# A planned one-core kernel (conv block, Fourier mixer, FFN): unread products on TensorE, FFN roundings on another engine, and other buffers for the last image

## The chip, the cores and the metric

One Trainium2 chip; the kernel uses one of its cores. The metric is the device time of one execution in microseconds (us). The kernel before was run three times: 4678.52, 4695.46 and 4697.34 us, so its median is 4695.46 us. A separate execution was profiled.

The core's engines work at the same time, each on its own stream of instructions, in order: TensorE (PE in the profile, with its weight loads as PEld) multiplies matrices into PSUM, VectorE (DVE) and ScalarE (ACT) do element-wise work, GpSimd (POOL) here only starts adding DMAs, and SyncE (SP) starts the other DMAs. TensorE's clock can be throttled; the profile gives the clock that was granted as a share of full speed.

## The reference

Input: 32 images of 96 channels, 56 x 56 pixels, float32. What is computed for each:

```python
# layer 0: inverted residual block
h = relu(bn(einsum('oc,bchw->bohw', w1, x)))        # 96 -> 576 channels
h = relu(bn(dwconv3x3(h, wdw)))                     # a 3x3 filter for each channel
x = x + bn(einsum('oc,bchw->bohw', w2, h))          # 576 -> 96
# layer 1: on tokens, t is [32, 3136, 96]
t = to_tokens(x)
t = t + attn(ln(t))     # 96 -> 192, relu, FFT over the tokens, a complex diagonal with relu,
                        # inverse FFT, 192 -> 96
t = t + ffn(ln(t))      # 96 -> 384 -> 96; inputs of both products are rounded to an 8-bit float
                        # (5 exponent, 2 mantissa bits), sums to a 16-bit float
x = from_tokens(t)
```

The two roundings to 8 bits inside the FFN (of the normalised input, and of the hidden values after the relu) are the "FFN roundings" of the title.

## The kernel before

**The stages of an image.** An image is worked in two halves of 28 rows in the conv block (`unit`, `last_channels`, `front`), in two halves of the spectrum in the Fourier mixer (`mid`), and in four quarters of 784 tokens in the inverse transform and the FFN (`back`).

- `unit`: 128 of the 576 channels of a half. Expand on TensorE (L584), relu into `hs` on ScalarE (L594), then the nine taps of the 3x3 filter: the first by ScalarE into `acc` (L610), one or two by ScalarE into `product` (L626), the others by VectorE (L637), and the products are added by a GpSimd DMA (L645). There are 7 `acc` buffers and 3 `product` buffers, each 128 x 1568 float32. `last_channels` does the last 64 channels on TensorE with banded matrices (L686, L722).
- `front`: the 576 -> 96 products and the residual in PSUM tile `pw` (L844, L878), copied out by ScalarE (`xt`, L891), normalised, kept in DRAM (`tdr`), turned, projected to 192 (L963), first step of the Fourier transform (L994), sent to DRAM (`ydr`).
- `mid`: loads a transform matrix `wb` (L1037, one buffer) and the data `yb` (L1045, two buffers), products on TensorE (L1073), the diagonal and the relus on ScalarE and VectorE (L1085 to L1120), the projection (L1159, L1171) and an inverse step (L1198 to L1202), sent to DRAM (`gdr`).
- `back`: loads `wd` (L1248, one buffer), `gd` (L1251, one buffer) and the residual `tt` (L1257, two buffers), the last inverse step on TensorE (L1272), added to `tt` by VectorE (L1277). Then `norm`: seven statistics (L788), eleven operations on 112 x 7 numbers, ten of them on VectorE and the square root on ScalarE (L798), with small tiles under the token `normf` (two sets). Then the first rounding: seven ScalarE instructions of 112 x 96 (L1289) into `u8`. Seven products turn it (L1307), ScalarE copies (`uT`, L1311). For each of three groups of hidden channels: products (L1328), copy to float16 on ScalarE (L1340), bias and relu on VectorE (L1346), second rounding on ScalarE (L1352, 128 x 784). Then the second FFN product (L1369), a copy (L1378), a bias (L1381), the sum with the residual on TensorE (L1388, which reads `tt` and lets it go, and L1399), a copy (L1404) and the store (L1407).

**What sets the order.** All of that is recorded as steps, each with an engine, a cost in us, the steps it follows, buffer tokens that it takes and gives back, and a rank. `Plan.emit` then plays the steps through a small event model in which each engine is free or busy: a free engine is given the ready step of lowest rank whose tokens are free. The order in which the model gives them out is the order of the instructions on each engine. Ranks come from `START` and `PACE`: `back` of image i has the rank of the conv block of image i + 3, so that several images are in work at once. The consequence at the end: when the conv block of the last image is done, the four quarters of each of the last three images' `back` remain, beside the last mixers.

**Tiles.** PSUM has three buffers `ps` from a pool, and `pw` is taken from another pool, one buffer, every time `front` needs it (`128, 2, 4, 128`, of which the last 32 columns of each 128 are not used).

## Time and profile before

| | |
|---|---|
| time, median of 3 runs (lowest to highest) | 4695.46 us (4678.52 to 4697.34) |
| the profiled execution: its time | 4682.55 us |
| the profiled execution: span from the first to the last instruction | 4680.7 us |
| mean granted TensorE clock | 0.967 |
| busy: PE, DVE, ACT, POOL | 4397.9, 4299.8, 4170.2, 337.3 us |
| steady images: time from one image to the next | about 140 us |

How to read the profile: the busy time of an engine is given as a sum and a share of the span; a second view cuts the span into 40 equal slices and gives the busy share of each in tenths. Groups of instructions are named by line, engine, operation, output tile and input tiles, with shapes, count, total busy time and mean duration. The chain that ended last is found from the last instruction backwards: at each step to what released it. In the list of waits, a row names who waited, who released it, the total, the number of times and the longest. A window is a stretch in us from the start of the span, with the busy time of each engine in it, the granted clock, and the share of the DMA engines. A float32 product of one instruction in the code is two matmul instructions in the profile, unless it is a transpose.

### The profile page before, as it was taken

The page shows a single profiled execution, that of the slowest core. Times are in us where ns is not written, and L with a number is a line of the kernel's source. Part 1 is how long each engine was busy: PE and PEld are TensorE (multiplying, and loading weights), DVE is VectorE, ACT ScalarE, POOL GpSimd, SP SyncE. Part 2 cuts the span into 40 slices and gives each one's busy share as a digit, 9 for nine tenths or more (in the row PEclk, how much of TensorE's full clock was granted, in tenths as well). Part 3 has the DMA queues.
Part 4 walks back from the last instruction along what each step waited for, and adds up shares of the span by engine and source line. Part 5 has one row for each costly group of instructions (what it writes and reads, how often), then busy time and mean ns, then how long its engine had stood idle before and what let it go on. Part 6 is the DMA issues. An engine that isn't in the chain of part 4 may idle for free.

```text
span 4680.7 us, 85686 instructions
## 1 busy us (share of the span) xinstructions
PE 4397.9 (94%) x33744; PEld 3205.3 (68%) x33744; DVE 4299.8 (92%) x6933; ACT 4170.2 (89%) x5510; POOL 337.3 (7%) x397
## 2 busy tenths in 40 slices
PE   7889999999999999999999999999999999999986
PEld 4567776676676767676777676676776776676774
DVE  8999999999999999999999999999999999999943
ACT  4777999999999999999999999998998999899976
POOL 0000000000000000000000000000000000000000
PEclk7999999999999999999999999999999999999987
DMA  4667777767776767776767777777776776777752
GB/s 97 135 158 172 183 179 171 178 167 171 178 175 166 186 163 185 177 181 167 180 170 176 183 176 169 181 176 171 184 182 166 181 179 163 184 178 175 170 135 78
DMA packets 390887, 789.28 MB, mean 169 GB/s; under 512 B 135600, under 2 KB 236532, under 8 KB 390484
## 3 DMA queue, kind: packets, MB, share of 16 engines
q1 hardware_dynamic: 335028, 479.15, 36.4%
q0 software_dynamic: 55296, 304.64, 33.6%
q8 instruction: 266, 4.36, 0.4%
q14 instruction: 137, 1.12, 0.1%
q10 hardware_dynamic: 160, 0.01, 0.0%
HBM read 286.38 MB, written 192.68 MB: 102 GB/s over the span
## 4 chain that ended last, share of the span: by engine, by line
PE 46%; ACT 14%; DVE 11%; DMA 6%; issue 2%; SPq 0%; POOLq 0%; ACTq 0%; DVEq 0%
PE pw L844 10%; PE ps L584 8%; DVE acc L637 7%; DMA acc<-product 5%; PE ps L722 4%; PE ps L1073 3%; PE ps L994 2%; PE ps L963 2%; PE ps L1369 2%; PE ps L1272 2%; PE ps L1171 2%; ACT acc L654 2%; PE ps L1328 2%; ACT product L626 1%; ACT acc L610 1%
## 5 line engine op out<-in xcount | busy, mean ns | idle before, releaser
L637 DVE SCALAR_TENSOR_TENSOR acc<-hs,wdw,acc 128x1540 f32<-128x1540 f32 (+2 forms) x1664 | 2971.6, 1793 | 27.2 <-ACT acc L610 18.6
L584 PE MATMUL ps<-xs,w1T 96*128 96x406 f32 x2048 | 823.4, 526 | 48.8 <-ACT al L751 11.6
L844 PEld LDWEIGHTS pw<-w2T,acc 128*112 128x112 f32 x7168 | 766.4, 181 | 64.3 <-issue 40.3
L844 PE MATMUL pw<-w2T,acc 128*112 128x96 f32 x7168 | 804.9, 267 | 5.0 <-ACT acc L654 4.8
L626 ACT ACTIVATE product<-hs,wdw 128x1568 f32<-128x1568 f32 (+1 forms) x384 | 609.4, 1591 | 14.5 <-DMA product<-product 14.1
L584 PEld LDWEIGHTS ps<-xs,w1T 96*128 96x128 f32 x2048 | 371.2, 195 | 300.0 <-issue 136.0
L594 ACT ACTIVATE hs<-ps,b 128x812 f32<-128x812 f32 x512 | 478.6, 935 | 97.8 <-PE ps L584 83.2
L645 POOL DMA_DIRECT2D acc<-product x256 | 227.7, 890 | 3306.4 <-DVE acc L637 384.9
L654 ACT ACTIVATE acc<-acc 128x1568 f32<-128x1568 f32 x256 | 386.9, 1512 | 63.8 <-DMA acc<-product 63.5
L610 ACT ACTIVATE acc<-hs,bd,wdw 128x1568 f32<-128x1568 f32 x256 | 435.2, 1700 | 5.5 <-DVE eo L498 5.4
L722 PE MATMUL ps<-hl,band 128*64 128x385 f32 (+3 forms) x3072 | 419.3, 498 | 4.5 <-ACT hs L594 2.3
L963 PE MATMUL ps<-watt,xnT 97*120 97x192 f32 x1792 | 350.3, 341 | 44.3 <-DVE V L1102 31.4
L963 PEld LDWEIGHTS ps<-watt,xnT 97*120 97x120 f32 x1792 | 305.2, 190 | 105.4 <-DVE V L1102 40.2
L1289 ACT ACTIVATE u<-tt,mf,rf 112x96 fp8e5<-112x96 f32 x896 | 346.4, 462 | 6.1 <-DVE mf L820 5.9
L1352 ACT ACTIVATE h<-h 128x784 fp8e5<-128x784 f16 x384 | 329.4, 860 | 22.3 <-DVE h L1346 21.1
L1073 PEld LDWEIGHTS ps<-wb,yb 112*128 112x128 f32 (+1 forms) x3584 | 306.9, 167 | 58.5 <-issue 23.9
L1340 ACT ACTIVATE h<-ps 128x784 f16<-128x784 f32 x384 | 315.4, 824 | 26.8 <-PE ps L1328 25.7
L1073 PE MATMUL ps<-wb,yb 112*128 112x112 f32 (+1 forms) x3584 | 330.7, 273 | 4.0 <-ACT hs L594 1.8
L722 PEld LDWEIGHTS ps<-hl,band 128*64 128x64 f32 (+1 forms) x3072 | 154.7, 135 | 204.1 <-issue 168.8
L1346 DVE TENSOR_SCALAR h<-h,b1q 128x784 f16<-128x784 f16 x384 | 160.8, 419 | 122.0 <-ACT h L1340 119.9
L994 PE MATMUL ps<-z,wa 56*64 56x384 f32 (+1 forms) x2048 | 242.6, 510 | 24.3 <-ACT hs L594 18.2
L1328 PE MATMUL ps<-uT,w1q 96*128 96x392 fp8e5 x768 | 196.9, 341 | 26.5 <-ACT xnT L948 9.5
(148 smaller groups left out, 6395.6 us busy)
## 6 DMA issues: line engine op xcount, KB each, us to landing
acc<-product POOLq DMA_DIRECT2D x256, 784.0 KB, 8.5
product<-product POOLq DMA_DIRECT2D x128, 756.0 KB, 10.7
yb<-ydr SPq DMA_DIRECT2D x256, 294.0 KB
wd<-in_wd_dram SPq DMA_DIRECT2D x128, 349.1 KB
wb<-in_wb_dram SPq DMA_DIRECT2D x64, 686.0 KB
ydr<-ya SPq DMA_DIRECT2D x256, 168.0 KB
xs<-in_x_dram SPq DMA_DIRECT2D x64, 609.0 KB
tdr<-xt SPq DMA_DIRECT2D x64, 588.0 KB
```

The source lines that it names most:

```text
L584: nc.tensor.matmul(u[h][:, j, 0:QW], lhsT=w1T[:, 128 * k : 128 * (k + 1)], rhs=xs[img, s][0:C, at : at + QW], start=True, stop=True,)
L594: nc.scalar.activation(flat[:, 2 * h * QW : 2 * (h + 1) * QW].rearrange("p (j w) -> p j w", j=2), u[h][:, :, 0:QW], AF.Relu, bias=b1[:, k ...
L610: nc.scalar.activation(acc[img, s, k], u["hs"][:, o + up : o + up + R, :], AF.Identity, scale=weight(up, 0), bias=bd[:, k : k + 1],)
L626: nc.scalar.activation(u["p", dr][:, ra:rb, :], u["hs"][:, ra + o + dr : rb + o + dr, :], AF.Copy, scale=weight(dr, 0))
L637: nc.vector.scalar_tensor_tensor(dst, src, weight(dr, dc), dst, ALU.mult, ALU.add)
L654: nc.scalar.activation(acc[img, s, k], acc[img, s, k], AF.Relu)
L722: nc.tensor.matmul(pv[:, :, ca:cb], lhsT=band[rows, j, dc + 1, 64 * o : 64 * o + 64], rhs=H[rows, q : q + 7, ca + dc : cb + dc], skip_grou ...
L844: nc.tensor.matmul(u["pw"][0:SK, t, n % 4, 0:C], lhsT=src[rows, (G * t + n) * SK : (G * t + n + 1) * SK], rhs=rhs, skip_group_check=True, **k,
L963: nc.tensor.matmul(pv[0:PK, q - a, 0:HA], lhsT=xnT[:, q, 0:PK], rhs=watt, start=True, stop=True,)
L994: nc.tensor.matmul(u["y", b][64 * c : 64 * c + n, j, 0 : 2 * HA], lhsT=wa[at, 0:n], rhs=rhs, start=True, stop=True)
L1073: nc.tensor.matmul(o, lhsT=lhsT, rhs=u["wb"][:, G * s + q, :], start=True, stop=True)
L1289: nc.scalar.activation(u["u8"][:, q, :], u["t"][:, q, :], AF.Identity, scale=u["r"][:, q : q + 1], bias=u["m"][:, q : q + 1], saturate=False,)
```

## The change

It has three parts.

1. **Unread products.** `pw` becomes one tile of 128 x 2 x 512, taken once; `front` uses the first 384 columns of each half. A new function `filler` multiplies `ident` by `ident` into the last 128 columns of the first half; nothing reads them. In `Plan.emit`, when TensorE is free in the model, no step is ready for it, steps are still to come, and it was busy for less than 0.75 of the last 3.413 us of the model, a filler is emitted and counted as 0.23 us of TensorE work. One more such product opens the group.
2. **Roundings.** In the `back` of the last three images (`TAIL = 3`) both FFN roundings are VectorE instructions (`tensor_scalar` and `tensor_copy`) in place of ScalarE ones, with costs in the model of 0.16 and 0.34 us.
3. **Buffers for the last image.** The last image's second `mid` takes its `wb` and both `yb` from `acc` buffers, and its quarters 2 and 3 of `back` take `tt` and the small tiles of `norm` from a `product` buffer each.

The instructions that result: 931 fillers and one opening product. Of the fillers, 187 stand before the expansion of the fourth image, 516 between that and the last expansion of the last image, and 228 after it. They come in runs of 1 to 35. On ScalarE 84 + 36 roundings are gone, on VectorE 84 + 36 are new. One load of `wb`, four of `yb` and two of `tt` have another destination. Because the model's clock and its free times change, the order of the steps changes on PE, ACT, DVE and SP in all of the program, not only where a filler stands.

```diff
+SPARSE = 0.75
+FILLER = 0.23
+TAIL = 3
 class Plan:
+    def sparse(self, now):
+        self.recent = [r for r in self.recent if r[1] > now - self.WINDOW]
+        return sum(b - max(a, now - self.WINDOW) for a, b in self.recent) < SPARSE * self.WINDOW
 ...
     def emit(self):
+        work = sum(s.engine == "PE" for s in self.steps)
 ...
                     cost = self.stretched(now, s.cost) if engine == "PE" else s.cost
+                    if engine == "PE":
+                        self.recent.append((now, now + cost))
+                        work -= 1
 ...
+                if engine == "PE" and idle[engine] and work and now > 0 and self.sparse(now):
+                    self.filler()
+                    idle[engine] = False
+                    cost = self.stretched(now, FILLER)
+                    self.recent.append((now, now + cost))
+                    heapq.heappush(events, (now + cost, count, engine, None))
+                    count += 1
 ...
+    pw = psw.tile([128, 2, 512], F32, name="pw", tag="pw")
 ...
+    def spare(name, p, n):
+        t = w1.tile([128, R, S], F32, name=name, bufs={"acc": 7, "product": 3}[name])
+        return t.rearrange("p r c -> p (r c)")[0:p, 0:n]
 ...
     def norm(u, tag, n, p, after, shift, take, give):
         def sums():
+            if "spare" in u:
+                at = G * C
+                u["st"] = u["spare"][:, at : at + 6 * n].rearrange("p (q v) -> p q v", v=6)
+                at += 6 * n
+                u["w"], u["sd"], u["d"], u["r"], *m = (u["spare"][:, at + n * v : at + n * v + n] for v in range(5))
 ...
                 if i % 4 == 0:
-                    u["pw"] = psw.tile([128, 2, 4, 128], F32, name="pw", tag="pw")
+                    u["pw"] = pw[:, :, 0 : 4 * C].rearrange("p t (q c) -> p t q c", c=C)
 ...
     def mid(img, half):
+        last = img == nimg - 1 and half == 1
+            if last:
+                u["wb"] = spare("acc", SK, 2 * G * SK).rearrange("p (k m) -> p k m", m=SK)
+                if last:
+                    u["yb", t] = spare("acc", SK, G * HA).rearrange("p (g h) -> p g h", h=HA)
 ...
     def back(img, h):
+        tail = img >= nimg - TAIL
+        last = img == nimg - 1 and h >= 2
+        TT, NF = ("product", []) if last else ("tt", ["normf"])
+            if last:
+                u["spare"] = spare("product", SK, R * S)
+                u["t"] = u["spare"][:, 0 : G * C].rearrange("p (q c) -> p q c", c=C)
 ...
+                    if tail:
+                        nc.vector.tensor_scalar(o, t, r, m, ALU.mult, ALU.add, saturate=False)
+                    else:
+                        nc.scalar.activation(o, t, AF.Identity, scale=r, bias=m, saturate=False)
+        engine, cost = ("DVE", 0.16) if tail else ("ACT", 0.36)
 ...
+                if tail:
+                    nc.vector.tensor_copy(u["h8"][:, c, :], u["h", c], saturate=False)
+                else:
+                    nc.scalar.activation(u["h8"][:, c, :], u["h", c], AF.Copy, saturate=False)
+            engine, cost = ("DVE", 0.34) if tail else ("ACT", act(784, 0, 0.09))
 ...
+    def filler():
+        nc.tensor.matmul(pw[:, 0, 4 * C :], lhsT=ident, rhs=ident, start=False, stop=False, skip_group_check=True)
+    nc.tensor.matmul(pw[:, 0, 4 * C :], lhsT=ident, rhs=ident, start=True, stop=False, skip_group_check=True)
+    plan.filler = filler
```

More of the change, by code (lines that the diff above doesn't have):

```diff
@@ L167, in __init__ @@
         self.moving = []
+        self.filler, self.recent = None, []
     def stretched(self, now, work):
@@ L771, in chain, with norm @@
         return t
-    def norm(u, tag, n, p, after, shift, give):
+    def norm(u, tag, n, p, after, shift, take, give):
         stt = nc.vector.scalar_tensor_tensor
         def sums():
-            u["st"] = w2.tile([p, n, 6], F32, name=f"st{tag}")
-            u["w"], u["sd"], u["d"], u["r"], *m = (
-                w2.tile([p, n], F32, name=f"{v}{tag}") for v in ("w", "sd", "d", "r") + ("m",) * shift
-            )
+            if "spare" in u:
[4 more added lines that the diff above has]
+            else:
+                u["st"] = w2.tile([p, n, 6], F32, name=f"st{tag}")
+                u["w"], u["sd"], u["d"], u["r"], *m = (
+                    w2.tile([p, n], F32, name=f"{v}{tag}") for v in ("w", "sd", "d", "r") + ("m",) * shift
+                )
             u["m"] = m[0] if shift else None
@@ L798, in root @@
             nc.scalar.activation(u["sd"], u["w"], AF.Sqrt, scale=1.0 / C)
-        t = [step("DVE", 1.12, sums, after, [f"norm{tag}"])]
+        t = [step("DVE", 1.12, sums, after, take)]
         if n > G:
@@ L923, in front @@
         sent[img, s] = step("SP", 0.1, keep, ev, late=written(2 * SK * G * C))
-        t = norm(u, "a", RP, SK, ev, False, [])
+        t = norm(u, "a", RP, SK, ev, False, ["norma"], [])
         for j in range(2):
@@ L1035, in matrix @@
         def matrix():
-            u["wb"] = w1.tile([SK, 2 * G, SK], F32, name="wb")
+            if last:
+                u["wb"] = spare("acc", SK, 2 * G * SK).rearrange("p (k m) -> p k m", m=SK)
+            else:
+                u["wb"] = w1.tile([SK, 2 * G, SK], F32, name="wb")
             nc.sync.dma_start(
@@ L1042, in f @@
             def f():
-                u["yb", t] = w2.tile([SK, G, HA], F32, name="yb")
+                if last:
+                    u["yb", t] = spare("acc", SK, G * HA).rearrange("p (g h) -> p g h", h=HA)
+                else:
+                    u["yb", t] = w2.tile([SK, G, HA], F32, name="yb")
                 for ri in range(2):
@@ L1052, in mid @@
         after = [sent[img, "y", h] for h in range(4)] + mid_set
-        w = step("SP", 0.1, matrix, after[:1], ["wb"], late=read(2 * G * SK * SK))
+        WB, YB = ("acc", "acc") if last else ("wb", "yb")
+        w = step("SP", 0.1, matrix, after[:1], [WB], late=read(2 * G * SK * SK))
         yb = [
-            step("SP", 0.1, load(t), after, ["yb"], ["ydr"] * (half and t), late=read(SK * G * HA))
+            step("SP", 0.1, load(t), after, [YB], ["ydr"] * (half and t), late=read(SK * G * HA))
             for t in range(2)
@@ L1143, in mid @@
                 ["ps", "V", "eo", "brief"],
-                (["yb"] if part == 2 else []) + (["yb", "wb"] if part == 1 else []),
+                ([YB] if part == 2 else []) + ([YB, WB] if part == 1 else []),
             )
@@ L1255, in residual @@
         def residual():
-            u["t"] = w2.tile([SK, G, C], F32, name="tt")
+            if last:
+                u["spare"] = spare("product", SK, R * S)
+                u["t"] = u["spare"][:, 0 : G * C].rearrange("p (q c) -> p q c", c=C)
+            else:
+                u["t"] = w2.tile([SK, G, C], F32, name="tt")
             nc.sync.dma_start(out=u["t"].rearrange("p q c -> p (q c)"), in_=tdr[img][h // 2, :, G * C * (h % 2) : G * C * (h % 2 + 1)])
@@ L1264, in back @@
         res = step(
-            "SP", 0.1, residual, after[:1] + [sent[img, h // 2]], ["tt"], ["tdr"] * (h == 3), late=read(SK * G * C)
+            "SP", 0.1, residual, after[:1] + [sent[img, h // 2]], [TT], ["tdr"] * (h == 3), late=read(SK * G * C)
         )
@@ L1280, in back @@
         t = step("DVE", dve(G * C, 0.06), add, [t], [], ["ps"])
-        t = norm(u, "f", G, SK, [t], True, [])
+        t = norm(u, "f", G, SK, [t], True, NF, [])
         def quantize(a, b):
@@ L1288, in f @@
                 for q in range(a, b):
-                    nc.scalar.activation(
-                        u["u8"][:, q, :],
-                        u["t"][:, q, :],
-                        AF.Identity,
-                        scale=u["r"][:, q : q + 1],
-                        bias=u["m"][:, q : q + 1],
-                        saturate=False,
-                    )
-            return f
-        t = step("ACT", 0.36 * 4, quantize(0, 4), t, ["u8"])
-        t = step("ACT", 0.36 * 3, quantize(4, G), [t], [], ["normf"])
+                    o, t, r, m = u["u8"][:, q, :], u["t"][:, q, :], u["r"][:, q : q + 1], u["m"][:, q : q + 1]
+                    if tail:
+                        nc.vector.tensor_scalar(o, t, r, m, ALU.mult, ALU.add, saturate=False)
+                    else:
+                        nc.scalar.activation(o, t, AF.Identity, scale=r, bias=m, saturate=False)
+            return f
+        engine, cost = ("DVE", 0.16) if tail else ("ACT", 0.36)
+        t = step(engine, 4 * cost, quantize(0, 4), t, ["u8"])
+        t = step(engine, 3 * cost, quantize(4, G), [t], [], NF)
         def turn():
@@ L1351, in f @@
             def f():
-                nc.scalar.activation(u["h8"][:, c, :], u["h", c], AF.Copy, saturate=False)
+                if tail:
+                    nc.vector.tensor_copy(u["h8"][:, c, :], u["h", c], saturate=False)
+                else:
+                    nc.scalar.activation(u["h8"][:, c, :], u["h", c], AF.Copy, saturate=False)
             return f
@@ L1361, in back @@
             p = step("DVE", 0.34, bend(c), [p])
-            ends.append(step("ACT", act(784, 0, 0.09), quantized(c), [p], [], ["h16"]))
+            engine, cost = ("DVE", 0.34) if tail else ("ACT", act(784, 0, 0.09))
+            ends.append(step(engine, cost, quantized(c), [p], [], ["h16"]))
         def outer():
@@ L1413, in back @@
         t = step("DVE", 0.34, shift, [t])
-        t = step("PE", 1.08, total, [t], ["ps", "brief"], ["tt", "y16"])
+        t = step("PE", 1.08, total, [t], ["ps", "brief"], [TT, "y16"])
         t = step("ACT", 0.97, copied_out, [t], [], ["ps"])
```

## The prediction

> **What bounds the kernel now.** I read the page's head and slices first, then windows by stage, then the groups and the chain of the stage that stands out.

> ```profile
> span 4680.7 us, 85686 instructions
> PE 4397.9 (94%) x33744; PEld 3205.3 (68%) x33744; DVE 4299.8 (92%) x6933; ACT 4170.2 (89%) x5510; POOL 337.3 (7%) x397
> ...
> PE   7889999999999999999999999999999999999986
> ...
> DVE  8999999999999999999999999999999999999943
> ACT  4777999999999999999999999998998999899976
> ...
> PEclk7999999999999999999999999999999999999987
> ```

> In the middle three engines are each busy for nine tenths or more: no single one is the limit, and a little time given back on one is mostly met by another. Only the two ends have slack, and there the clock falls too. The windows (us; PE, PEld, DVE, ACT, POOL busy; granted clock; DMA share; GB/s) give sizes:

> ```profile
> 0.00:300.00 300.00, 239.24 (x1460) 156.28 (x1461) 265.60 (x315) 188.70 (x188) 27.92 (x42) 0.85 0.59 128
> 300.00:4430.00 4130.00, 3969.49 (x30990) 2901.62 (x30989) 3928.49 (x6270) 3803.82 (x5024) 308.55 (x354) 0.99 0.73 175
> ```

> ```profile
> 4430.00:4472.00 42.00, 39.83 (x340) 34.08 (x340) 18.68 (x48) 30.31 (x50) 0.86 (x1) 0.92 0.61 146
> 4472.00:4610.00 138.00, 107.78 (x773) 85.39 (x772) 65.40 (x211) 102.99 (x175) 0.00 (x0) 0.85 0.44 118
> 4610.00:4681.00 71.00, 41.58 (x186) 27.95 (x183) 21.58 (x92) 44.41 (x76) 0.00 (x0) 0.62 0.26 73
> ```

> The conv block ends at 4472. The 209 us behind it, "the tail", have no full engine: they are dependent chains. Clock lost (length x (1 - clock)) is 45 us in the first 300, about 50 in the middle (4 us windows summed; the two digits above are too coarse) and 51 in the last 251. PE's idle time is 61, 161 and 62 us in the same three stretches.

> The tail's groups, and its chain (start us, us, what):

> ```profile
> L1289 ACT ACTIVATE u<-tt,mf,rf 112x96 fp8e5<-112x96 f32 x91 | 34.6, 458 | 2.8 <-DVE mf L820 2.7
> L1352 ACT ACTIVATE h<-h 128x784 fp8e5<-128x784 f16 x39 | 32.5, 853 | 6.6 <-DVE h L1346 5.8 <-DVE df L808 0.7
> ...
> L1346 DVE TENSOR_SCALAR h<-h,b1q 128x784 f16<-128x784 f16 x39 | 16.4, 420 | 65.1 <-ACT h L1340 65.0
> ```

> ```profile
> 4473.61 1.38 PE ps L1272 x14
> ...
> 4652.60 2.69 PE ps L1272 x14
> ...
> 4660.55 1.54 ACT u L1289 x4
> 4662.09 0.75 ACT h L1352
> 4662.89 1.47 PE ps L1369 x4
> ```

> The reader is to see that the same 14 matmuls of L1272 take 1.38 us at 4473 and 2.69 at 4652, and that both ScalarE roundings stand on the chain.

> **The change part by part.** The sum is made against the profiled execution: 4682.55 us, of which 4680.7 are the span. It is 13 us under the median of the three runs (4695.46), inside their spread of 19.

> *Part 1, what a filler costs.* Near row: seven float32 products of 112 x 112 (L1073 x14) take 1.55 us on the chain at full clock, 0.22 each; with 128 columns for 112 that is 0.25. So 187 fillers at the front are 47 us, 516 in the middle 129, 228 after the last expansion 57: in each stretch less than PE's idle time. Where a run is as long as the wait that it fills, it costs nothing; that wait is the cover. Without it each costs 0.25 us of PE (0.5 while the clock is halved), and behind it in PE's queue stands the next stage's matmul, and ScalarE waits for that one's eviction. Only three fillers wait for a semaphore (ScalarE's reading of `pw`), so they bring no new waiting.

> *What the clock is worth.* [...]

> Tail: I take the chain's PE pieces from 4430 on and subtract the same piece at full clock: L1272 three at 2.66 against 1.38, 3.9 us; L963 two at 4.8 against 2.28, 5.1; L1159 three at 2.88 against 1.55, 4.0; L1388 eight at 1.31 against 0.81, 4.0; L1369 six, 8.5 in all against 0.82 each, 3.6; L1171 0.9; L1328, L1399 and L945 together 3.5. Sum 25. Some windows will still be slow, since the plan doesn't know where the chip's windows begin: 20. Fillers on the path: 57 us against 62 of idle is tight, and the tail gets shorter; I charge one in seven, 8 us. Net 12.

> Middle: about 20 slow episodes, 50 us of lost clock; the whole chain is 46% PE, so 23 are worth something. One filler in four on work, 129 / 4 x 46%, costs 15. Net 8. The whole order is dealt anew too, which I can't price beyond +-20: 0.5% of the stretch.

> Front: VectorE is busy 266 of 300 us and covers PE; I can tie 7 us of its waits to a slow PE (264 to 272, 240 to 252) and charge 3 for fillers. Net 4. The first run of 24 fillers stands before the first expansion (9.21 us); at half clock it is up to 12 us long, but ScalarE takes that expansion's result at 19.20 only, since it waits on a DMA.

> *Part 2, roundings.* The window from 4430 holds all twelve quarters of the last three images (L1272 x168). ScalarE loses 84 instructions at 0.37 (seven take 2.61 us) and 36 at 0.86: 62 us of its 178. Unknown is VectorE's price. First rounding: seven L788 of the same 96 columns take 1.22 us; I take that, with ends 0.16 (what ten small numbers take) and 0.25 each. Second: nearest is L1346, 784 float16 to float16, 0.42. [...] I take 0.6. VectorE gets 15 + 22 = 37 us more on 106 of 251: it has the room.

> On the chain stand 15.5 us of L1289 and 17.3 of L1352. They become 15.5 x 1.22 / 2.61 = 7.2 and 17.3 x 0.6 / 0.86 = 12.1: gain 13.5. The copies queued behind them on ScalarE (L1340; 65 us of VectorE's waits) go sooner: 4 more. [...] Late next is VectorE: a rounding in front of a mixer's L1102 (1.03 us) now delays it. [...]

> *Part 3, buffers.* SyncE's queue shows what is removed:

> ```profile
> SPq L1248 <- PE ps L1272: 45.8, 11, 11.4
> SPq L1257 <- PE ps L1388: 40.8, 7, 10.1
> ```

> L1257 is the residual that waits for a `tt` to come free; behind it in SP's queue stand stores and the next `wd` and `gd`. The last image's L1272 start at 4616, 4625.5, 4641.3 and 4652.4. `wd` and `gd` for the third are issued at 4628.5, and the two quarters before show 5.6 and 6.4 us from the `gd` issue to L1272: it could start at 4635. The two waits of 15.8 and 11.1 us can then be some 9.5 each, as the first: 8 less; I count 7, ends 0 and 15. The `wb` and `yb` for the last mixer: those loads wait 15 us for PE (L1037, L1045), none of it on the chain: 0, ends 0 and 4.

> *Sum:* tail -12 - 17.5 - 7 = -36.5, middle -8, front -4: -48.5. 4682.55 - 48.5 = 4634. The runs shown lie 4 under to 15 over the profiled execution; the range has room for that.

> **Rivals.** (a) *The clock doesn't follow*: the chip's idle gaps fall elsewhere than the plan's, the granted clock stays near 0.97, and half of the fillers' charge of 8 + 15 + 3 us is left. For it: episodes come irregularly (936, 1384, 1664, 1920) while the plan's fillers are periodic. Against: in the tail runs of 4 to 19 stand in just the gaps of several us. Time: 4682.5 - 17.5 - 7 + 13 = 4671. (b) *Slower*: fillers stand in PE's way. The place is the middle, where PE has 4% idle. All gains without costs are 20 + 23 + 7 + 17.5 + 7 = 75. If PE sets the pace everywhere (not 46%), half of all 932 x 0.25 = 233 us on work costs 116: 4724. Point of turning: a third on work. Against: DVE and ACT are as full as PE and pay part of it. (c) *More than I count*: the middle's chains are PE's wherever the clock falls, all 50 come back, the tail gives its 25 of clock and 30 of rounding, the front its 4: 4682.5 - 50 - 55 - 4 = 4573. (d) *Nothing*: one bound gives way to DVE everywhere, 4683.

> **How the numbers follow.** Likeliest case 0.65 (4605 to 4660 alone), (a) 0.14, (b) 0.05, (c) 0.13, (d) 0.03. A measurement of this kernel tells about 0.5%, 23 us, from no change: faster is under 4672, slower over 4719. Faster: 0.65 + 0.13 + 0.08 of (a) = 0.86. Within: 0.06 of (a), (d), and 0.01 of (b) = 0.10. Slower: 0.04. The range leaves out half of (c) and (b), and the outer edges: 4585 to 4685.

> **What would show it.** Right: clock of the last 70 us at 0.9 or more, in place of 0.62; L1272 x14 near 1.4 us to the end; the second rounding 0.57 to 0.6 on VectorE; about 22 us less from the end of the conv block to the last mixer's store, and 15 less behind that; PE busy up by about 230 less the slow time, while the middle's step from image to image stays at 140 us or falls by 0.3. Wrong: matmuls waiting behind fillers with their data long there; VectorE full in the tail; a second rounding near 1 us; a middle that moves by more than 20 us either way.

## The result, and the profile after

| | before | after |
|---|---|---|
| time, median of 4 runs (lowest to highest) | 4695.49 us (4678.52 to 4697.34) | 4647.06 us (4644.14 to 4653.59) |
| ratio of the means, 95% interval | | 0.9907 (0.9882 to 0.9932) |
| profiled span | 4680.7 us | 4642.4 us |
| mean granted clock | 0.967 | 0.994 |

The median fell by 48.4 us, and the forecast was a fall of 48.5, to 4634 us from a profiled execution of 4682.55. The means fell by 43.8 us and the profiled executions by 38.4, so how near the two falls are depends on which figure is taken. Cut into stages, the profiled spans tell another story. The first stage ends with the fourth copy of a `pw` (line 891 before, 928 after), the tail begins with the last one (the forecast's own cuts were at 300 us and at 4430 to 4472 us, so its row is laid beside these stages only roughly):

| us | first image's conv block | middle | tail |
|---|---|---|---|
| before | 174.8 | 4297.3 | 208.6 |
| after | 192.9 | 4267.9 | 181.6 |
| difference | +18.1 | -29.4 | -27.0 |
| forecast | -4 | -8 | -36.5 |

The page of the kernel after, head and slices:

```profile
span 4642.4 us, 89413 instructions
...
PE 4496.0 (97%) x35608; PEld 3351.9 (72%) x35608; DVE 4335.3 (93%) x7053; ACT 4121.2 (89%) x5390; POOL 339.9 (7%) x397
...
PE   7999999999999999999999999999999999999998
...
DVE  7899999999999999999999999999999999999956
ACT  4677999999999999999999999999999999999854
...
PEclk8999999999999999999999999999999999999999
```

The clock's last two digits are 9 and 9 where they were 8 and 7, and its first is 8 where it was 7. PE is busier by 98 us, though the span is shorter. In the last two slices VectorE has 5 and 6 where it had 4 and 3, ScalarE 5 and 4 where it had 7 and 6. The windows of the kernel after by stage, cut at 4461 (the end of the conv block) and at 4580 (the last mixer's last store), with the columns that the prediction named:

```profile
0.00:300.00 300.00, 255.22 (x1694) 181.16 (x1694) 247.66 (x288) 177.59 (x177) 25.71 (x39) 0.91 0.54 116
300.00:4430.00 4130.00, 4047.05 (x32246) 3005.07 (x32246) 3953.17 (x6312) 3834.16 (x5056) 314.16 (x358) 1.00 0.74 177
4461.00:4580.00 119.00, 110.61 (x962) 94.10 (x960) 85.87 (x275) 69.75 (x104) 0.00 (x0) 1.00 0.50 137
4580.00:4643.00 63.00, 52.16 (x413) 44.80 (x411) 37.61 (x143) 25.57 (x36) 0.00 (x0) 0.99 0.29 80
```

The granted clock is full or within 1% of it everywhere but in the first 300 us. Summed over windows of 4 us from 300 to 4428, the lost clock is 0.4 us; the same sum for the kernel before is 58. The clock's record in the two traces has the values 1.0 and 0.5 alone, and its changes are whole multiples of 3.413 us apart (80 stretches before, 16 after). From the conv block's end to the last mixer's store it is 119 us for 136 (SyncE's last such store is issued at 4607.9), and behind that 62 for 73.

The groups of the kernel after in its last 213 us:

```profile
L1486 PE MATMUL pw<-ident 128*128 128x128 f32 x422 | 54.0, 275 | 0.0
...
L1403 DVE CAST h<-h 128x784 fp8e5<-128x784 f16 x36 | 20.4, 565 | 0.8
...
L1343 DVE TENSOR_SCALAR u<-tt,rf,mf 112x96 fp8e5<-112x96 f32 x70 | 17.9, 323 | 0.4
```

Both roundings are on VectorE at 0.565 and 0.32 us, and the fillers are 54 us of PE. The chain of the kernel after near its end (start, us, what):

```profile
4607.57 0.56 DVE u L1343 x2
...
4609.49 1.45 PE ps L1324 x14
...
4616.26 0.82 PE ps L1423 x4
4617.08 0.67 PE pw L1486 x6
4617.75 1.24 PE ps L1357 x7
...
4620.02 1.38 PE ps L1324 x14
...
4632.59 0.58 DVE h L1403
...
4636.03 0.89 PE pw L1486 x8
4636.92 0.67 PE ps L1442 x7
```

The 14 matmuls of the inverse step (L1324 now) keep to 1.4 us up to the end; before they had grown to 2.69. The reader is also to see the price: at 4617.08 six instructions of fillers and at 4636.03 eight stand on the chain, directly ahead of matmuls that the end needs. Taken over the whole tail, such pieces are 8.9 us. SyncE's waits in the tail of the kernel after (us in total, times, longest):

```profile
SPq L1296 <- PE ps L1324: 32.3, 8, 6.7
...
SPq L1309 <- PE ps L1453: 22.3, 6, 5.9
...
SPq L1309 <- PE ps L1442: 6.6, 2, 3.4
```

From the conv block's end on, before, the loads of `wd` waited 42.1 us for PE and those of the residual 53.4 (27.6 for L1388, 25.8 for L1399, which are L1442 and L1453 now). They wait 32.3 and 28.9.

### The profile page after: what moved, and what is told of

It is laid out like the page before. It is cut to its first block, busy times and chain, and to the rows that moved or that the text cites. A ratio compares the mean times of both kernels' runs of the same rounds, so it can differ in the third digit from the quotient of the medians.

```text
span 4642.4 us, 89413 instructions
## 1 busy us (share of the span) xinstructions
PE 4496.0 (97%) x35608; PEld 3351.9 (72%) x35608; DVE 4335.3 (93%) x7053; ACT 4121.2 (89%) x5390; POOL 339.9 (7%) x397
## 4 chain that ended last, share of the span: by engine, by line
PE 56%; ACT 14%; DVE 14%; DMA 5%; issue 3%; SPq 0%; DVEq 0%; ACTq 0%; POOLq 0%
PE pw L881 14%; PE ps L615 9%; DVE acc L668 7%; PE ps L1118 4%; PE ps L1031 3%; PE ps L1000 3%; PE ps L1324 3%; ACT product L657 3%; DMA acc<-product 3%; PE ps L1216 2%; PE ps L753 2%; PE ps L1378 2%; PE pw L915 2%; PE ps L1423 2%; PE ps L717 1%
## 5 line engine op out<-in xcount | busy, mean ns | idle before, releaser
L615 PE MATMUL ps<-xs,w1T 96*128 96x406 f32 x2048 | 805.3, 515 | 18.7 <-ACT hs L625 13.7
L881 PEld LDWEIGHTS pw<-w2T,acc 128*112 128x112 f32 x7168 | 749.4, 178 | 63.6 <-issue 44.5
L1000 PE MATMUL ps<-watt,xnT 97*120 97x192 f32 x1792 | 334.1, 330 | 16.7 <-DVE V L1147 13.4
L1000 PEld LDWEIGHTS ps<-watt,xnT 97*120 97x120 f32 x1792 | 292.5, 183 | 71.9 <-issue 35.8
L1118 PEld LDWEIGHTS ps<-wb,yb 112*128 112x128 f32 x3528 | 296.6, 165 | 52.2 <-issue 16.0
L1390 ACT ACTIVATE h<-ps 128x784 f16<-128x784 f32 x384 | 315.5, 824 | 15.4 <-PE ps L1378 10.1
L1405 ACT ACTIVATE h<-h 128x784 fp8e5<-128x784 f16 x348 | 298.8, 859 | 34.0 <-DVE h L1396 33.7
L1118 PE MATMUL ps<-wb,yb 112*128 112x112 f32 x3528 | 321.2, 270 | 5.8 <-ACT h L1390 2.5
L1345 ACT ACTIVATE u<-tt,mf,rf 112x96 fp8e5<-112x96 f32 x812 | 315.2, 463 | 0.6 <-DVE mf L857 0.6
L1486 PE MATMUL pw<-ident 128*128 128x128 f32 x1862 | 268.2, 283 | 3.4 <-ACT xt L928 3.4
L1486 PEld LDWEIGHTS pw<-ident 128*128 128x128 f32 x1862 | 247.4, 197 | 24.9 <-issue 12.5
```

The source lines that it names most:

```text
L615: nc.tensor.matmul(u[h][:, j, 0:QW], lhsT=w1T[:, 128 * k : 128 * (k + 1)], rhs=xs[img, s][0:C, at : at + QW], start=True, stop=True,)
L881: nc.tensor.matmul(u["pw"][0:SK, t, n % 4, 0:C], lhsT=src[rows, (G * t + n) * SK : (G * t + n + 1) * SK], rhs=rhs, skip_group_check=True, **k,
L1000: nc.tensor.matmul(pv[0:PK, q - a, 0:HA], lhsT=xnT[:, q, 0:PK], rhs=watt, start=True, stop=True,)
L1118: nc.tensor.matmul(o, lhsT=lhsT, rhs=u["wb"][:, G * s + q, :], start=True, stop=True)
L1390: nc.scalar.activation(u["h", c].rearrange("p (j w) -> p j w", j=2), u["H", c][:, :, 0:n], AF.Copy)
L1486: nc.tensor.matmul(pw[:, 0, 4 * C :], lhsT=ident, rhs=ident, start=False, stop=False, skip_group_check=True)
```

## The experiments

The questions: is it the products' work on the clock that moved the middle, or the order that the planner dealt with them? Where do the front's 18 us come from? What is each part worth in the tail, alone and together? And what does a filler cost? All ratios are to the kernel before. Stages come from one profiled execution each; the middles of the four kernels planned without fillers lie between 4297 and 4314, which is how well a middle is known. Tails are known better: the kernel after and two others with its roundings, its buffers and a held clock in the tail (experiments 2 and 6) have 181.6 to 182.9. The time of each kernel is a median; its ratio is to runs of the kernel before that were made beside it, whose medians were 4691.36 to 4697.98.

**1. The order without the products.** The plan is dealt as if there were fillers, and none is issued; the unread products but the opening one are what is left out.

```diff
     def filler():
-        nc.tensor.matmul(pw[:, 0, 4 * C :], lhsT=ident, rhs=ident, start=False, stop=False, skip_group_check=True)
+        pass
```

> The plan counts its 931 fillers as in the change, so every other instruction stands in the changed kernel's order, but no filler is issued (the opening product stays). Theory 1, the products themselves hold the clock: the granted clock falls back to about 0.97, the 20 or so slow episodes of the middle return, and the middle (end of the first image's conv block to end of the last one's) is back near the kernel before, 4297 us, not 4268; the tail keeps what the roundings give and loses some 15 to 20 us; time about 4680. Rival, the new order is what helped: clock near 0.97 and yet a middle of about 4268 and a time of about 4645 to 4655.

Measured: 4704.86 us, ratio 1.0015 (1.0002 to 1.0028); stages 191.8, 4317.3, 202.5. Its window of the middle:

```profile
300.00:4430.00 4130.00, 3986.94 (x30872) 2909.21 (x30872) 3919.67 (x6238) 3800.66 (x4997) 310.77 (x355) 0.98 0.73 174
```

The same order with its products (the kernel after) is 49.4 us shorter in the middle and 20.9 in the tail, and 1.1 us longer in front. So the order itself brought nothing: the middle is 20 us longer than before, where about the same was expected, and longer than that of any kernel planned without fillers. What shortened the middle is the work of the products: this order loses 101 us of clock from 192 to 4428 (4 us windows), and the kernel after 4. (Experiment 5 tells the clock from the mere presence of the products.) And 17 of the front's 18 us are there without a single product: they come with the order. The five kernels without fillers also stand nearly in the order of their lost clock: with 58, 61, 67, 75 and 89 us of clock lost from 300 to 4428 their middles are 4297, 4310, 4308, 4314 and 4317.

**2. Fillers from 20 us of the plan on.** This takes the first run of 24 out of the plan, and the plan's account of it too.

```diff
-                if engine == "PE" and idle[engine] and work and now > 0 and self.sparse(now):
+                if engine == "PE" and idle[engine] and work and now > 20 and self.sparse(now):
```

> The change, with fillers allowed only from 20 us of the plan on: the run of 24 ahead of the first expansion is gone. Theory 1, that run delays the first expansion by 5 us and deals ScalarE's first DMAs behind late setup loads, 18 us in the first image: the first image's conv block ends near 175 us in place of 192.9, the rest stays, time about 4630. Rival, later runs of the front (18 and 35 fillers) cost it: the first image ends at 185 or later and the time stays within 8 us of the changed kernel's 4647.

Measured: 4636.13 us, ratio 0.9883 (0.9854 to 0.9913); stages 177.0, 4282.2, 181.7. The front gives back 16 of its 18 us, as expected; the middle is 14 longer than in the kernel after, no more than two dealings of the order may differ by, and as a whole the two ratios overlap. ScalarE's own order in the first 35 us shows the place. Before (start, us, line, idle before it):

```profile
10.85 0.28 ACT L406 ACTIVATE V<-V 128x96 f32<-128x96 f32 x1 [6.62 <-DVE V L405]
14.06 5.09 ACTq L458 DMA_DIRECT2D shb<-yb  x3
19.20 2.59 ACT L594 ACTIVATE hs<-ps,b 128x812 f32<-128x812 f32 x3 [8.07 <-DMA shb<-yb]
```

After:

```profile
15.94 0.94 ACT L625 ACTIVATE hs<-ps,b 128x812 f32<-128x812 f32 x1 [11.80 <-PE ps L615]
16.77 0.27 ACT L432 ACTIVATE V<-V 128x96 f32<-128x96 f32 x1
30.10 2.35 ACTq L484 DMA_DIRECT2D shb<-yb  x3
32.50 1.77 ACT L625 ACTIVATE hs<-ps,b 128x812 f32<-128x812 f32 x2 [15.46 <-DMA shb<-yb]
```

The order without the products:

```profile
11.07 0.94 ACT L625 ACTIVATE hs<-ps,b 128x812 f32<-128x812 f32 x1 [6.66 <-PE ps L615]
11.90 0.27 ACT L432 ACTIVATE V<-V 128x96 f32<-128x96 f32 x1
15.10 10.51 ACTq L484 DMA_DIRECT2D shb<-yb  x3
25.66 1.77 ACT L625 ACTIVATE hs<-ps,b 128x812 f32<-128x812 f32 x2 [13.49 <-DMA yb<-in_a_b_dram]
```

And with fillers from 20 us on:

```profile
10.93 0.28 ACT L432 ACTIVATE V<-V 128x96 f32<-128x96 f32 x1 [6.63 <-DVE V L431]
14.14 5.34 ACTq L484 DMA_DIRECT2D shb<-yb  x3
19.53 2.59 ACT L625 ACTIVATE hs<-ps,b 128x812 f32<-128x812 f32 x3 [8.32 <-DMA shb<-yb]
```

Before, ScalarE does the square root (L406, 432 now) first, issues three small DMAs (`shb`) and then takes the expansion's results. With the first run in the plan, one copy of an expansion's result is put ahead of the square root. That copy waits for the expansion, which is behind the fillers in the kernel after (14.37 us for 9.21); the square root comes 6 us later, VectorE waits 6.3 us for it, and the DMAs go out at 30.10 for 14.06, in the midst of SyncE's small setup loads. Behind them stand ScalarE's next copies and, on PE, the next expansions, which wait 13.5 us. Without the products the square root is only 1 us late, and still the DMAs take 10.5 us for 5.1, and the copy behind them starts at 25.66. Why these three DMAs are let go so late the semaphores in the traces of before and after show, which the views leave out. In both, SyncE's setup loads and these DMAs carry the eight semaphores 100 to 103 and 106 to 109 in turn, and on ScalarE's queue a wait for its own semaphore stands ahead of each of the three (101, 106, 108 before; 108, 100, 102 after). In the kernel after the wait of the first ends at 30.03, with the landing of a `w2a` load that was issued at 25.65, and that of the third at 31.87, with a `cw` load issued at 29.66. Before, the third's ends at 18.57, with `yb<-in_a_g_dram`, issued at 9.40. Without the products the profile names `yb<-in_a_b_dram`, two loads later, as the one that ended ScalarE's wait, and the last of the three ends at 25.61. So with each order these DMAs were tied to other loads. How 6.5 us at 25 us became 17 at the end of the stage was not followed.

**3. Each part alone and in pairs.** Six kernels and the two that were there make all eight combinations. Fillers alone:

```diff
-        last = img == nimg - 1 and half == 1
+        last = False
...
-        tail = img >= nimg - TAIL
-        last = img == nimg - 1 and h >= 2
+        tail = False
+        last = False
```

> Fillers alone: roundings on ScalarE and buffers as before. Theory 1: front +18 and middle -29 as in the change, tail from 208.6 us to about 192 (clock alone 16 to 20), clock 0.99, time about 4668. Rival, the tail is won by the roundings only: tail stays within 5 us of 208.6 although its clock is near 1, time about 4680.

Roundings and buffers, no fillers planned or issued:

```diff
-                if engine == "PE" and idle[engine] and work and now > 0 and self.sparse(now):
+                if False and engine == "PE" and idle[engine] and work and now > 0 and self.sparse(now):
```

> Roundings on VectorE and buffers of the change, no fillers in plan or program (but the opening product). Theory 1: front and middle as before within 15 us, tail 208.6 to about 192, clock 0.97, time about 4678. Rival, roundings and buffers do nearly all of the tail's 27 us: tail at 182 to 186 and time about 4668.

Fillers and buffers, the roundings on ScalarE (`tail = False` alone):

```diff
-        tail = img >= nimg - TAIL
+        tail = False
```

> The change without the roundings (both on ScalarE as before), with fillers and the last image's buffers. Theory 1: buffers are worth 7 us, so the tail is 199 (fillers alone) less 7: about 192, time about 4656. Rival, the buffers do nothing without the roundings: tail 197 or more, time about 4662.

Fillers and roundings, the old buffers (`last = False` in `mid` and `back`):

```diff
-        last = img == nimg - 1 and half == 1
+        last = False
...
-        last = img == nimg - 1 and h >= 2
+        last = False
```

> The change without the last image's buffers, with fillers and roundings. Theory 1: the tail is 181.6 plus 7, about 188, time about 4654. Rival, the roundings and the clock gain the same without the buffers: tail 184 or less, time within 4 us of 4647.

Roundings alone, which is the edit of the second of these with `last = False`:

```diff
-                if engine == "PE" and idle[engine] and work and now > 0 and self.sparse(now):
+                if False and engine == "PE" and idle[engine] and work and now > 0 and self.sparse(now):
...
-        last = img == nimg - 1 and h >= 2
+        last = False
```

> The kernel before with the roundings of the last three images on VectorE alone: no fillers (one opening product), no other buffers. Theory, as forecast: tail 208.6 less 17, about 191, first image and middle as before within 15 us. Rival, the slow clock leaves less: tail 197 or more, since PE at half clock is what the quarters wait for.

Buffers alone, the same with `tail = False` instead:

```diff
-                if engine == "PE" and idle[engine] and work and now > 0 and self.sparse(now):
+                if False and engine == "PE" and idle[engine] and work and now > 0 and self.sparse(now):
...
-        tail = img >= nimg - TAIL
+        tail = False
```

> The kernel before with the last image's other buffers alone: no fillers (one opening product), roundings on ScalarE. Theory, as forecast: tail 208.6 less 7, about 202. Rival, without the other two parts the buffers do nothing: tail 207 or more.

Measured (F fillers, R roundings, B buffers; the last column is the tail's difference to before):

| | time, us | ratio (95%) | first | middle | tail | |
|---|---|---|---|---|---|---|
| none (before) | 4695.49 | 1 | 174.8 | 4297.3 | 208.6 | |
| F | 4661.91 | 0.9935 (0.9914 to 0.9956) | 193.6 | 4271.5 | 199.0 | -9.6 |
| R | 4673.12 | 0.9960 (0.9946 to 0.9975) | 175.0 | 4313.7 | 191.9 | -16.7 |
| B | 4687.27 | 0.9995 (0.9983 to 1.0007) | 174.9 | 4307.9 | 206.6 | -2.0 |
| F R | 4655.08 | 0.9915 (0.9896 to 0.9934) | 192.5 | 4271.9 | 188.4 | -20.2 |
| F B | 4652.73 | 0.9909 (0.9890 to 0.9928) | 190.8 | 4271.6 | 187.7 | -20.9 |
| R B | 4669.82 | 0.9954 (0.9931 to 0.9978) | 174.2 | 4309.6 | 184.2 | -24.4 |
| F R B (after) | 4647.06 | 0.9907 (0.9882 to 0.9932) | 192.9 | 4267.9 | 181.6 | -27.0 |

Three things follow. First, the first stage: 16 to 19 us more wherever fillers are planned from the start, nowhere else. Second, the middle: the four with fillers lie within 4 us of each other at 4271, the four without at 4307 on the mean, so it is the fillers that the middle answers to, with 36 us. Third, the tail: its gains do not add, though the total hides it. Alone the three come to 9.6 + 16.7 + 2.0 = 28.3, near the 27.0 that they give together. But fillers and roundings give 6.1 us less than their sum, fillers and buffers 9.3 more, roundings and buffers 5.7 more, and these nearly cancel. The roundings give 16.7 alone and 6.1 as the last part, the fillers 9.6 and 2.6; the buffers give 2.0 alone, 7.7 behind the roundings and 11.3 behind the fillers. The buffers alone make no difference that the ratio can tell.

Against what was expected: the fillers alone gave 9.6 for 16 to 20; for roundings with buffers the rival held (tail 182 to 186), and for the buffers alone nearly so (207 or more); fillers with buffers did better than expected (187.7 for 192); roundings alone (191.9 for 191) and the kernel without the buffers (188.4 for 188) came as expected.

The buffers alone did do what they were made for. The last three starts of the inverse step are 12.4, 9.1 and 9.4 us apart, where 9.7, 15.8 and 11.1 stood before, and the last quarter starts 6.3 us earlier in the tail. But it then needs 32.6 us to the end for 28.3. The chain there, L1405 being the second rounding and L1390 and L1458 copies, is ScalarE with no gap:

```profile
4668.22 0.75 ACT h L1405
4668.97 0.71 ACT h L1390
4669.68 0.71 ACT o L1458
4670.38 0.75 ACT h L1405
```

The window of the tail without fillers (roundings and buffers), and with fillers alone:

```profile
4483.74:4667.90 184.16, 141.21 (x955) 108.03 (x955) 123.58 (x415) 94.22 (x138) 0.00 (x0) 0.82 0.40 113
```

```profile
4465.14:4664.10 198.96, 171.68 (x1432) 149.14 (x1431) 88.08 (x304) 147.67 (x252) 0.00 (x0) 0.97 0.42 111
```

The first has a clock of 0.82 for 184 us, 33 us of lost clock; filling it brings 1.00 and 2.6 us of time. Adding up the pieces of the chain over the tail says where it goes:

| chain over the tail, us | PE | of it fillers | DVE | ACT | DMA |
|---|---|---|---|---|---|
| none (before) | 91 | | 37 | 67 | 0 |
| F | 51 | 11.5 | 40 | 78 | 12 |
| R B | 92 | | 49 | 18 | 12 |
| F R B (after) | 89 | 8.9 | 62 | 20 | 0 |

With fillers alone the chain moves over to ScalarE, whose roundings are still there. With all three, ScalarE's share is down to 20 us, but VectorE has 62 and the fillers 9: against roundings and buffers alone, PE's own work on the chain is some 12 us less, and VectorE has taken that up.

**4. What a filler costs: twice as many.** The kernel after's order, each filler issued twice.

```diff
     def filler():
         nc.tensor.matmul(pw[:, 0, 4 * C :], lhsT=ident, rhs=ident, start=False, stop=False, skip_group_check=True)
+        nc.tensor.matmul(pw[:, 0, 4 * C :], lhsT=ident, rhs=ident, start=False, stop=False, skip_group_check=True)
```

> The changed kernel in its own order, each filler issued twice: 233 us of PE work more. Theory 1, the fillers already fill most of PE's idle time (93 us left in the middle, 19 in the tail), so more than half of the second ones land on work and about half of that on the chain: middle 50 to 80 us longer, tail 15 to 25, time about 4730. Rival, they stand in waits that are longer than planned: under 20 us in all, time under 4667.

Measured: 4747.59 us, ratio 1.0113 (1.0095 to 1.0132); stages 217.9, 4320.7, 206.2. That is 18 us over the 4730 expected; the front was not in that sum. The groups of the two lines:

```profile
L1486 PE MATMUL pw<-ident 128*128 128x128 f32 x1862 | 369.5, 280 | 2.7 <-ACT xt L928 2.7
...
L1487 PE MATMUL pw<-ident 128*128 128x128 f32 x1862 | 362.7, 277 | 0.0
```

How many fillers the kernel after has in each of its three stages (two instructions each), and one run of 14 instructions in it:

```profile
0.00:192.91 192.91, 38.75 (x286) 38.15 (x286) 0.88 0.48 103
192.91:4460.80 4267.89, 175.43 (x1154) 157.08 (x1154) 1.00 0.74 175
4460.80:4642.40 181.60, 54.01 (x422) 52.19 (x422) 1.00 0.43 118
```

```profile
4549.30 1.72 PE L1486 MATMUL pw<-ident 128*128 128x128 f32 x14
```

Shorter runs of the same form take 0.38 us for two instructions and 1.05 for eight (experiment 2, at 4552.63 and 4556.90): from two to 14 they are 1.34 us for six more fillers, 0.22 each. The length of a run, 0.25 for each of seven, has some 0.15 us in it that do not grow with the count. These stages hold 143, 577 and 211 fillers (187, 516 and 228 were counted at other cuts). So the second fillers are some 32, 129 and 47 us more (an estimate at full clock), and the stages grew by 25.0, 52.8 and 24.6: about 78% in front, 41% in the middle, 52% in the tail. The waits are mostly used up by the first fillers; of the second ones half is paid over the whole kernel (102 of 208 us). PE's share of the chain is 74%, where it was 46% before and 56% after.

**5. Shorter fillers: 64 columns in place of 128.** The order of the kernel after.

```diff
-        nc.tensor.matmul(pw[:, 0, 4 * C :], lhsT=ident, rhs=ident, start=False, stop=False, skip_group_check=True)
+        nc.tensor.matmul(pw[:, 0, 4 * C : 4 * C + 64], lhsT=ident, rhs=ident[:, 0:64], start=False, stop=False, skip_group_check=True)
```

> The changed kernel in its own order, each filler with 64 columns for 128, so half as long. Theory 1, the fillers that fall on work cost some 15 us in the middle and 8 in the tail, and the clock needs only part of the cover: clock 0.985 or more, half of that cost comes back, time about 4636 to 4642. Rival, the clock follows how long PE is busy: clock 0.98 or less, slow episodes return, middle over 4280, time over 4655.

Measured: 4679.35 us, ratio 0.9966 (0.9951 to 0.9981); stages 217.0, 4283.1, 185.6, all longer than after. The expectation failed at its start: the product is not half as long, the 1862 instructions of the fillers are busy for 269.9 us (288 ns as a mean) against 268.2 (283 ns) with 128 columns. And the clock doesn't hold under it. A window in the tail of this kernel, all of it and then the fillers alone (in the second PE, PEld, clock, DMA share, GB/s):

```profile
4630.00:4650.00 20.00, 19.50 (x129) 17.43 (x128) 12.54 (x53) 5.16 (x8) 0.00 (x0) 0.78 0.38 98
```

```profile
4630.00:4650.00 20.00, 10.24 (x73) 10.39 (x72) 0.78 0.38 98
```

PE counts as busy for 19.5 of 20 us, 10.2 of them fillers, and the granted clock is 0.78. In the first 110 us it is 0.71, as in the order without products (0.71), against 0.81 after. So the clock does not follow the busy time of the profile: of two fillers that are busy nearly as long, in the same order, the one with more moving columns held it better (0.994 over the span for 0.981). What exactly is counted these runs don't show. They do show that the gain is the clock's and not that of having products there: with as many of them, the clock over the span is 0.981 for 0.994 and the kernel 32 us slower by the medians.

**6. Narrower weights: 64 of 128, fillers from 20 us on.**

```diff
-        nc.tensor.matmul(pw[:, 0, 4 * C :], lhsT=ident, rhs=ident, start=False, stop=False, skip_group_check=True)
+        nc.tensor.matmul(pw[0:64, 0, 4 * C :], lhsT=ident[:, 0:64], rhs=ident, start=False, stop=False, skip_group_check=True)
```

> Fillers from 20 us of the plan on, each with 64 columns of weights for 128 (64 partitions of output), 128 moving columns as before. Theory, the clock follows the columns that stream and not the time that weight loads take, as the run with 64 moving columns suggests: clock 0.985 or more, time within 10 us of the run with fillers from 20 us on (4636), and a filler not shorter than 0.22 us. Rival, the clock follows the number of cells in use: clock 0.98 or less, time over 4660.

Measured: 4650.66 us, ratio 0.9908 (0.9886 to 0.9930), not told apart from 0.9883 (0.9854 to 0.9913) with full weights, though 15 us over it by the medians where within 10 was expected; stages 178.1, 4291.8, 182.9. One run of fillers with each (start, us, form, count), narrow first:

```profile
4558.79 1.41 PE L1486 MATMUL pw<-ident 128*64 128x128 f32 x11
```

```profile
4556.90 1.05 PE L1486 MATMUL pw<-ident 128*128 128x128 f32 x8
```

Eleven in 1.41 us and eight in 1.05 are 0.13 for each instruction: fewer weight columns saved nothing here, and the clock held (0.993 over the span, 0.991 with full weights).

**7. Fewer fillers.** If the clock needs less than is spent on it, a lower threshold is better. With 0.65 for 0.75 the plan issues 428 fillers instead of 888, from 20 us on.

```diff
-SPARSE = 0.75
+SPARSE = 0.65
...
-                if engine == "PE" and idle[engine] and work and now > 0 and self.sparse(now):
+                if engine == "PE" and idle[engine] and work and now > 20 and self.sparse(now):
```

> Fillers from 20 us of the plan on, and only where the plan's TensorE was busy for less than 0.65 of its last window, for 0.75: 428 in place of 888. Theory, a filler on the chain costs two fifths of its time, so half as many save some 20 us where the clock holds: clock 0.985 or more, time about 4620 to 4630. Rival, the cover gets too thin: clock 0.98 or less, slow episodes of the middle return, time over 4650.

Measured: 4598.31 us (4594.33 to 4608.91), ratio 0.9804 (0.9782 to 0.9825): under both kernels, clear of the 0.9883 with twice the fillers, and 22 us under the lowest time that was expected. Stages 171.6, 4245.0, 175.6. Its page and its group of fillers:

```profile
span 4592.2 us, 87386 instructions
...
PE 4411.9 (96%) x34602; PEld 3249.2 (71%) x34602; DVE 4330.2 (94%) x7053; ACT 4115.2 (90%) x5390; POOL 340.2 (7%) x397
```

```profile
L1486 PE MATMUL pw<-ident 128*128 128x128 f32 x856 | 128.0, 286 | 1.3 <-ACT xt L928 1.3
```

The clock is 0.991 with half the fillers, as it is with 888. From 300 to 4428 it loses 10 us, where 16 are lost with 888 from 20 us on; in the tail it loses 7, where the other loses none, and the tail is 6 us shorter all the same. PE is busy 92 us less, and in the tail only 2.7 us of fillers stand on the chain. The 460 fillers less are about 103 us at 0.22, the time is 38 us less: 37%, near what doubling showed for the middle. But the order was dealt anew here too, and this order was not run without its fillers: how much of the 38 us is the order's is not shown.

## Why the prediction was right in total, and where it was not

The mechanism was right: the products held the clock (0.994 for 0.967), and the roundings and buffers shortened the tail (184.2 us for 208.6 without fillers). Its sum came out to the microsecond because misses offset each other. Between the profiled executions the front took 22 us more than its step said (+18.1 for -4), the tail gave 9.5 less, and the middle gave 21 more; that is 10 us too little between the two profiled executions (38.4 for 48.5). The medians stand 13 us over the profiled time before and 3 us over it after, and that difference of 10 closed the gap: the hit to the microsecond is chance.

- *A filler's length*: taken as the length of a run, 0.25 held (14 instructions in 1.72 us). On PE one more costs 0.22 (1.34 us for six), so all 931 are 208 us and not 233.
- *The first run of 24 is harmless, since ScalarE takes that result at 19.20 only*: this step failed. It looked at when a result is read and not at what the planner would do with its account of the run: one copy went ahead of the square root, and the DMAs, 16 us later, took the front along. The prediction's "new order, +-20" was given to the middle alone.
- *Middle, -8*: the mechanism was right, the size not. Lost clock was 58 us from 300 to 4428 (the prediction had about 50), and 0.4 is left. In one and the same order, 97 us of lost clock less and 129 us of fillers more make -49. If no more than the 97 came back, the fillers cost at most 48, 37% of their length; if they cost no less than nothing, at least 51% came back. The prediction took 46%, the share of PE in the whole chain, of 50 us: the 50 was too small, and by these two profiles the 46% too. Those profiles differ by 69 us and the medians by 58, so the bounds are rough. That PE is on the chain more often where the clock is low would explain a larger share, but was not measured by itself. The charge of 15 us lies inside the bound.
- *The clock's whole loss*: a mean of 0.967 over 4680.7 us is 154 us of lost clock, and not all of it came back: the kernel of experiment 7 loses about 100 us of clock less than the one with roundings and buffers and no fillers, and is 71.5 us faster (4669.82 and 4598.31), in another order and net of its fillers.
- *Tail, fillers -12*: they gave 9.6 alone and 2.6 as the last part. The sum of slow PE pieces, 25 us, describes the chain before; with roundings and buffers in place, what PE gave up on the chain, some 12 us, VectorE took, and 33 us of lost clock were worth 2.6 net of the fillers. The charge of 8 us for fillers on the path was right (8.9).
- *Roundings -17.5*: 16.7 alone, 6.1 as the last. The second takes 0.565 us. No run showed the 0.6 that the sum uses for it, nor the 0.57 that is named beside it as a sign: both were the author's estimates, and near. The nearest row (0.42) was too low. Nor does a run show the 30 us of rounding in rival (c): alone the roundings gave 16.7. The first takes 0.25 in a run of seven (1.77 us at 4648.62 with roundings and buffers, where 1.22 was taken and 0.25 each was the upper end), which costs 0.55 us more for each of the runs on the chain.
- *Buffers -7*: 6.8 as the last part, but 2.0 alone. The starts of the last image's quarters are 9.7, 9.2 and 10.5 us apart, where 9.5 were said and 9.7, 15.8 and 11.1 stood before: the step was right, but alone it only moved the wait to ScalarE.
- *The places in the tail*: 22 and 15 us less ahead of and behind the last mixer's store were said, and 17 and 10 came.

So rival (a), a clock that doesn't follow, fell at once; (c), more than is counted, came true in part in the middle and nowhere else. Of rival (b), fillers in the way, the doubled fillers show the mechanism: with 208 us of fillers more the kernel is 1.1% slower than before, so the turning point lies between one filler and two in each place.

In the tail 8.2 of the 9.5 us missing are in the single sizes (9.6, 16.7 and 2.0 alone for 12, 17.5 and 7) and 1.3 in the adding. But that the adding cost so little is luck too. The prediction took three gains from one and the same chain, which had 158 us of PE and ScalarE, and did not ask what each was worth when the others were there: pairs gave from 6.1 us less to 9.3 more than their sums.

## What to carry to other kernels

Unread products can pay where TensorE is on the chain just when the clock falls: here the clock went from 0.967 to 0.994, and the middles with fillers are 36 us shorter (4271 for 4307). But on an engine that is busy for 97% half of each further product was paid (102 of 208 us; two fifths in the middle), so it is worth trying fewer: 428 here held the clock over the span as well as 888, though the order changed with them. When a planner counts what is added, its order changes even where the addition itself is harmless: compare with the same order without the addition before a stage's gain or loss is put down to it. Gains that are read off one chain need not add, and a total near their sum does not show that they do; as the last of three, one part was worth a quarter of what it gave alone, another three times as much.

## What the runs showed of the hardware that was not expected

- The unread float32 products with 64 moving columns were busy nearly as long as those with 128 (1862 instructions in 269.9 and 268.2 us), and did less for the clock: 0.981 for 0.994 over the span, 0.78 in a stretch in which PE counts as busy for 98%. With 64 weight columns for 128 an instruction took the same 0.13 us (eleven in 1.41, eight in 1.05), and the clock was 0.993 for 0.991.
- Rounding 112 x 96 float32 to 8 bits took VectorE 0.25 us in a run of seven (1.77 us; 323 ns as a mean of its records), where 2.61 us for seven stood on ScalarE.
- Three small DMAs at the start, issued from ScalarE, took 10.5 us to be let go for 5.1, without any change to them. In the traces of before and after each stands behind a wait for its own one of eight semaphores, which an earlier SyncE load carries too, and the order decides which load that is (the last wait ended at 18.57 before and at 31.87 after).
